# Convolution-offset sampling, attention and expert layer on one core: a one-sided row ramp, two alternating PSUM pairs, transposed exponentials, and elementwise work moved between engines

## The chip, the cores and the metric

The kernel runs on one core of one Trainium2 chip. The metric is the device time of one execution in microseconds (us): the median of three runs of the kernel before is 10409.05 us (10402.94 to 10426.91). The engines of the core are named as in the profile: PE is TensorE (PEld its weight loads, which overlap the matmuls), DVE is VectorE, ACT is ScalarE, POOL is GpSimd, and SP issues the DMAs.

## What is computed

The input is 16 images of 64 x 64 pixels with 128 channels. Layer 0 normalises groups of four channels, computes two offsets for every channel and pixel with a 3 x 3 convolution, and reads the normalised image at the shifted place by bilinear interpolation; the result is added to x. Layer 1 is an attention inside each token (eight heads of 16 numbers, a 16 x 16 score matrix for each head) and a layer of 64 experts, each of which takes its eight best tokens of the image.

```python
coords = off + grid                       # per channel and pixel: row c0, column c1
c0, c1 = clip(coords[0], 0, 63), clip(coords[1], 0, 63)
mapped = bilinear(group_norm(x), c0, c1)  # four neighbours, weights from the fractions
x = x + mapped
q, k, v = heads(layer_norm(x) @ w_qkv + b_qkv)
attn = softmax((q * scale)[..., :, None] * k[..., None, :], axis=-1)
x = x + einsum('bhlij,bhlj->bhli', attn, v) @ w_proj + b_proj
x = x + experts(layer_norm(x))            # top 8 tokens of each of 64 experts
```

## The kernel before

`image` (line 1034) emits the work of one image: image 0 by itself, images 1 to 14 as a hardware loop (line 1070), and image 15 by itself; `finish` then runs the experts. Each image has 256 steps (`SLOTS`), that is 128 pairs of steps. All work of an image is first recorded as a list of operations, each with a slot (its due step), and `order` (line 237) then plays the engines through with estimated costs (`weight`, line 194) and fixes the order of each engine's queue. The order in a queue is thus set when the program is built; on the chip an instruction only waits for its operands. The cost rule knows that a DVE operation with two SBUF operands, or an SBUF-to-SBUF scalar or copy operation, can't run beside POOL (`shared`, line 224).

Sampling (`sample`, line 685), for each pair `p`: four DMAs bring the column coordinates into `chat` (`load_cols`); two bf16 matmuls write row arguments into `rps` (`spread_rows`); two ACT passes turn them into row weights `rhat`, a Relu of the argument and then a Relu of 1 minus it (`ramp_rows`; every eighth pair takes one DVE instruction instead); ACT makes the column weights in place (`ramp_cols`); 64 small matmuls multiply the rows held in `xr` with `rhat` into `yps` (`mains`); DVE multiplies `yps` with `chat` into `prod` (`product`); and each second pair, eight matmuls add up `prod` in `acc` (`sums`). `rps` and `yps` are one pair of PSUM banks each; `acc`, `bank`, `bank2` and `cbank` are the other four banks. `chat` has four buffers, `rhat` three, `prod` three.

`prep` (line 505) makes the next image ready while the present one is sampled: statistics, `normalize` into `pad` (DVE), differences along the columns into `big` (`along`, two DVE instructions), and differences down the rows into the staging buffers `xl` (`down`, eight DVE instructions), from which DMAs write `xn_d` in HBM. `load_rows` (line 601) brings `xn_d` back into `xr` with 32 DMAs for an image. They can be issued once all of `xn_d` is written and the sampling has done with `xr`.

`tokens` (line 795) runs the attention for 512 tokens at a time, eight times an image. For each of four token groups: `qkv_mm` and `qkv_add`; `ends` finds the largest and the smallest key of a head (DVE); `scores` multiplies both with q (POOL, into `top` and `den`); a DVE maximum of the two is the largest score (line 904). Then, in two halves: `score` (two POOL instructions), `expo` (ACT exponential in place and DVE sum), `weigh` (POOL multiplies with v into the one buffer `ev`, DVE sums). `proj` multiplies with `w_proj`; POOL has added `b_proj` to the residual before (line 897). `layer_norm` (line 768) scales with four DVE instructions into `xln` where it feeds the experts.

Of the kernel before, what the change touches and what calls it, by code (L numbers as in the profile page):

```python
# [9 lines left out]
F32 = mybir.dt.float32  # L10
# [9 lines left out]
P = 128  # L20
# [12 lines left out]
REACH = 10.0  # L33
ROW0 = (0, 12, 20, 32)
# [3 lines left out]
NCHAT, NRHAT, NPROD = 4, 3, 3  # L38
# [102 lines left out]
class Work:  # L141
# [52 lines left out]
    def weight(self, op):  # L194
        total, cells, shape = 0, {}, None
        for fn, outs, ins in op.operands():
# [14 lines left out]
            elif op.lane == "gpsimd":  # L211
                total += 1000 if n <= NA else 150 + (6 if fn == "tensor_scalar" else 1.8) * n
# [89 lines left out]
class Images:  # L302
# [8 lines left out]
    def __init__(self, ctx, tc, x, conv_w, conv_b, w_qkv, b_qkv, w_proj, b_proj, gate_w, gate_b,  # L311
# [14 lines left out]
        self.rps = ps.tile([P, 2, 512], F32, name="rps")  # L326
        self.yp = ps.tile([P, 2, CHW], F32, name="yps")
        self.ys = [self.yp[:, 0, :], self.yp[:, 1, :]]
# [49 lines left out]
        self.one = keep([P, 1], "one")  # L378
        nc.vector.memset(self.one, 1.0)
# [16 lines left out]

        id16 = keep([16, 16], "id16", BF16)
# [8 lines left out]
        srow = keep([1, 2, WIN], "srow")  # L406
        nc.vector.tensor_scalar(srow[:, 0], self.iot[0:1, :WIN], -1.0, None, ALU.mult)
        nc.vector.tensor_scalar(srow[:, 1], self.iot[0:1, :WIN], 1.0, None, ALU.add)
        line = self.big.bitcast(BF16)[0:1, 6144:].rearrange("p (r t c) -> p r t c", r=2, t=8)
        self.sel = [keep([P, 8, P], f"sel{o}", BF16) for o in range(2)]  # L410
        for o in range(2):
            sel = self.sel[o].rearrange("p t (a h i) -> p t a h i", a=2, h=2)
            for a in range(2):
                for h in range(2):
                    nc.vector.tensor_scalar(
                        sel[:, :, a, h], bcast(pat[:, 16 * a + h : 16 * (a + 1) : 2], 2, WIN),
                        (1.0, -1.0)[o], None, ALU.mult)
            nc.vector.tensor_copy(
                line[:, 0].rearrange("p t (q i) -> p (t q) i", i=WIN),
                bcast(srow[:, o], 1, 32))  # L420
            nc.vector.memset(line[:, 1], (-1.0, 1.0)[o])
# [67 lines left out]
        self.rstd = [keep([P, NA], f"rstd{i}") for i in range(2)]  # L489
        self.qkv = keep([P, NA, 3, C], "qkv")  # L490
# [5 lines left out]
        self.ev = keep([P, 4, HD, HD], "ev")  # L496
# [8 lines left out]
    def prep(self, b, turns, slot, norm_slot):  # L505
# [41 lines left out]
        def group5():  # L547
# [3 lines left out]
            nc.gpsimd.tensor_tensor(gmv[:, 3:4], gmv[:, 3:4], self.half[:, 0:1], ALU.pow)  # L551

# [3 lines left out]
        def normalize(t):  # L556
            nc.vector.tensor_scalar(
                self.pad[:, 1 + 8 * t : 9 + 8 * t, 1 : 1 + IMG],
                self.big[:, CHW * t : CHW * (t + 1)].rearrange("p (i j) -> p i j", j=IMG),
                gmv[:, 2:3], gmv[:, 3:4], ALU.subtract, ALU.mult,  # L560
            )
# [6 lines left out]
        def along(s):  # L568
            if s == 0:
                nc.vector.tensor_tensor(  # L570
                    big[:, :, : mid - 1], pin[:, :, : mid - 1], pin[:, :, 1:mid], ALU.subtract)
                nc.scalar.copy(big[:, :, mid - 1 : mid + 1], pin[:, :, mid - 1 : mid + 1])
            else:
                nc.vector.tensor_tensor(
                    big[:, :, mid + 1 :], pin[:, :, mid + 1 :], pin[:, :, mid : IMG - 1],
                    ALU.subtract)

        def down(r):
            st = self.xl[:, r % 2].rearrange("p a c -> p (a c)").rearrange(
                "p (i j) -> p i j", j=IMG)  # L580
# [694 lines left out]
```

## Time and profile before

The profiled execution took 10408.53 us; its span, from the first to the last instruction, is 10406.5 us. The program divides so (times from the start of the span):

| stretch, us | what runs | length, us |
|---|---|---|
| 0 to 82 | constants, preparation of image 0 | 82 |
| 82 to 655 | image 0 | 573 |
| 655 to 9185 | loop over images 1 to 14 | 14 x 609 |
| 9185 to 9790 | image 15 | 605 |
| 9790 to 10406 | `finish` | 616 |

POOL's first instruction of a loop pass starts at 1264.34 us and, twelve passes later, at 8578.33 us, which makes 609.5 us for an image. The groups of instructions in one pass (4914.3 to 5525.0 us) that the change bears on, each with its count, its busy time in that pass and the mean of one:

| engine, tile | count | busy us | mean ns |
|---|---|---|---|
| ACT second pass rhat<-rhat,one | 112 | 128.6 | 1148 |
| ACT first pass rhat<-rps | 112 | 113.5 | 1013 |
| DVE rhat<-rps | 16 | 19.4 | 1216 |
| DVE pad<-big,gmv | 8 | 6.3 | 846 |
| DVE big<-pad | 2 | 4.5 | 2258 |
| DVE xl<-big | 8 | 12.2 | 1672 for seven, 615 for the last |
| POOL ev<-sc,qkv | 64 | 151.5 | 2367 |
| POOL sc<-sc,top | 64 | 125.8 | 1965 |
| POOL t<-t,bproj | 8 | 11.2 | 1394 |
| PE bank<-wproj,tr | 64 | 10.2 | 307 |

In the profile all of an image's instructions carry line 188, where the recorded operations are emitted; they are told apart by their tiles. `out<-in` names the tile written and those read.

### The profile page before, as it was taken

To read this page: it belongs to the slowest core of one execution; us is meant where nothing else is said; L and a number is where in the kernel's file an instruction comes from. 1 tells how busy PE (TensorE), PEld (TensorE's weight loads), DVE (VectorE), ACT (ScalarE), POOL (GpSimd) and SP (SyncE) were. 2 spreads that over 40 slices of the span, in tenths; PEclk is the share of its full clock that TensorE was granted. 3 is DMA by queue.
4 is the path that set the end of the run, shared out by engine and by line. 5 is a ranking of instruction groups with operands and counts; after the bars stand their busy time and mean duration, and the time that the engine had idled before them with its cause. 6 is when DMAs were issued, how large, how long until landed. Compare 5 with 4: busy or idle time off the path is not lost. (4 is left out here: it accounts for less than half of the span.)

```text
span 10406.5 us, 367626 instructions
## 1 busy us (share of the span) xinstructions
PE 8673.1 (83%) x156228; PEld 4367.3 (42%) x156228; DVE 8475.8 (81%) x11691; ACT 7657.4 (74%) x8034; POOL 7911.5 (76%) x5666
## 2 busy tenths in 40 slices
PE   7978788797878889788888978788897878888567
PEld 3434344343434434343443434344343434434247
DVE  5988889888888988888898888889888888988712
ACT  5878788787878878787887878788787878878500
POOL 3978788787878878787887878788787878878700
PEclk9999899998989999999999999999998999999755
DMA  6565555555555555555555555555555555555277
GB/s 160 160 166 157 159 159 158 160 161 163 158 158 159 153 161 159 163 160 160 158 154 161 159 162 161 158 152 156 164 160 159 162 158 154 157 163 157 79 213 247
DMA packets 1325857, 1672.20 MB, mean 161 GB/s; under 512 B 441632, under 2 KB 658464, under 8 KB 1322080
## 3 DMA queue, kind: packets, MB, share of 16 engines
q1 hardware_dynamic: 1303904, 1613.24, 54.4%
q10 hardware_dynamic: 20224, 34.61, 0.9%
q8 instruction: 1244, 20.38, 0.9%
q14 instruction: 485, 3.97, 0.1%
HBM read 1378.16 MB, written 268.96 MB: 158 GB/s over the span
## 5 line engine op out<-in xcount | busy, mean ns | idle before, releaser
L188 DVE SCALAR_TENSOR_TENSOR prod<-chat,yps 128x1024 f32<-128x1024 f32 x2048 | 2470.7, 1206 | 552.7 <-PE yps L188 254.6
L188 PE MATMUL yps<-rhat,xr 32*32 32x176 f32 (+1 forms) x131072 | 2621.3, 282 | 347.7 <-DVE prod L188 324.8
L188 POOL TENSOR_TENSOR ev<-sc,qkv 128x1024 f32<-128x1024 f32 x1024 | 2429.5, 2373 | 546.3 <-ACT sc L188 484.2
L188 PEld LDWEIGHTS yps<-rhat,xr 32*32 32x32 f32 x131072 | 1860.2, 106 | 1692.0 <-DVE prod L188 926.2
L188 PE MATMUL cbank<-pad,wconv 128*128 128x512 f32 x4608 | 2433.2, 626 | 39.1 <-DVE far L188 15.4
L188 ACT ACTIVATE rhat<-rps 128x1024 f32<-128x1024 f32 x1792 | 1815.9, 1013 | 633.1 <-PE rps L188 526.8
L188 POOL TENSOR_TENSOR sc<-sc,top 128x1024 f32<-128x1024 f32 x1024 | 2010.4, 1963 | 231.6 <-DVE top L188 203.2
L188 ACT ACTIVATE rhat<-rhat,one 128x1024 f32<-128x1024 f32 x1792 | 2057.6, 1148 | 47.1
L188 POOL TENSOR_TENSOR sc<-qkv 128x1024 f32<-128x1024 f32 x1024 | 1987.9, 1942 | 68.9 <-DVE qkv L188 67.6
L188 PE MATMUL rps<-parts,sel 128*128 128x512 bf16 x4096 | 1251.0, 387 | 723.9 <-ACT rhat L188 414.1
L188 DVE TENSOR_REDUCE den<-sc 128x64 f32<-128x1024 f32 x1024 | 1239.8, 1211 | 326.2 <-ACT sc L188 323.0
L188 DVE TENSOR_REDUCE att<-ev 128x64 f32<-128x1024 f32 x1024 | 1233.3, 1204 | 314.1 <-PEq L1070 265.8
L188 ACT ACTIVATE sc<-sc 128x1024 f32<-128x1024 f32 x1024 | 1071.7, 1047 | 497.9 <-PEq L1070 315.1
L188 ACT ACTIVATE chat<-chat,cbi,csc 128x1024 f32<-128x1024 f32 x1024 | 1255.6, 1232 | 125.8 <-DMA chat<-cc_d 108.8
L188 ACT ACTIVATE chat<-chat,cbi 128x1024 f32<-128x1024 f32 x1024 | 1161.4, 1139 | 183.8 <-DMA chat<-cc_d 162.5
L188 PE MATMUL acc<-prod,red 128*32 128x512 f32 x8192 | 1155.4, 629 | 8.5 <-DVE prod L188 8.5
L188 PEld LDWEIGHTS cbank<-pad,wconv 128*128 128x128 f32 x4608 | 828.4, 193 | 692.6 <-issue 468.1
L188 PEld LDWEIGHTS <-sel 128*128 128x128 bf16 x4096 | 334.3, 98 | 1819.4 <-issue 1564.2
L188 POOL TENSOR_TENSOR top<-qkv,kmm 128x128 f32<-128x128 f32 x512 | 226.2, 442 | 692.0 <-POOLq L1070 359.1
L188 DVE TENSOR_SCALAR xln<-t,mv,rstd 128x128 f32<-128x128 f32 x512 | 530.0, 1094 | 41.8 <-POOL rstd L188 41.8
L188 PE MATMUL bank<-wqkv,tr 128*128 128x384 f32 x1024 | 487.3, 561 | 30.8 <-ACT tr L188 18.1
L188 DVE RECIPROCAL den<-den 128x128 f32<-128x128 f32 x512 | 480.0, 937 | 4.5
(143 smaller groups left out, 8134.9 us busy)
## 6 DMA issues: line engine op xcount, KB each, us to landing
chat<-cc_d SPq DMA_DIRECT2D x8192, 128.0 KB
xr<-xn_d SPq DMA_DIRECT2D x512, 128.0 KB
xn_d<-xl SPq DMA_DIRECT2D x192, 256.0 KB
pc_d<-pc SPq DMA_DIRECT2D x128, 384.0 KB
parts<-pc_d SPq DMA_DIRECT2D x768, 64.0 KB
xl<-in_x_dram SPq DMA_DIRECT2D x128, 256.0 KB
xres<-in_x_dram SPq DMA_DIRECT2D x256, 128.0 KB
cc_d<-cd SPq DMA_DIRECT2D x128, 256.0 KB
```

The lines of the kernel that those rows point to most:

```text
L188: getattr(engine, fn)(*args, **kwargs)
```

## The change

1. Rows: before, a row's weight is 1 minus the distance to it, cut to between 0 and 1, by way of a ramp that is cut at both ends, and `xn_d` holds first differences down the rows. After, a row window of 32 is described from its middle (`MID` = 16): one row is held whole, the two first differences beside it, and for the rest second differences, each difference with a ramp that is cut at zero alone. `ramp_rows` is one ACT Relu for every pair; `by_vector` is never true.
2. Banks: `rps` and `yps` become two pairs of PSUM banks, taken in turn by the pairs; a pair's row arguments and, after them, its products are written to the same banks. `rhat` has two buffers.
3. Preparation: `normalize` goes from DVE to ACT, `along` from DVE to POOL, and `down` is replaced by `first` (eight POOL instructions, in place) and `second` (eight POOL instructions into the staging buffers), with `middle` and `sides` for the rows at the middle. Two small POOL instructions are added for the mean times the scale.
4. Layer norm: `scale` goes from DVE to ACT, with two small POOL instructions added.
5. Attention: the smallest key is subtracted from the keys (`shift`, POOL), so that the largest score is the Relu of q times the largest shifted key (`tops`, POOL, then ACT). `expo` writes its result transposed, so that `ev` is laid out by key and then by query; `weigh` works in place on it, and the two DVE sums read it with a step of 16 numbers. `ev` has two buffers.
6. `b_proj` is added by four matmuls in `proj`, and the POOL addition is dropped.

The general path for far offsets (`general`, line 1078) keeps the old differences with `dense`; it isn't taken with these inputs.

```diff
+MID = 16
...
-NCHAT, NRHAT, NPROD = 4, 3, 3
+NCHAT, NRHAT, NPROD = 4, 2, 3
...
-                total += 1000 if n <= NA else 150 + (6 if fn == "tensor_scalar" else 1.8) * n
+                total += 1000 if n <= NA else 150 + (6 if fn == "tensor_scalar" else 1.75) * n
...
-        self.rps = ps.tile([P, 2, 512], F32, name="rps")
-        self.yp = ps.tile([P, 2, CHW], F32, name="yps")
-        self.ys = [self.yp[:, 0, :], self.yp[:, 1, :]]
+        self.yps = [ps.tile([P, 2, CHW], F32, name=f"yps{i}") for i in range(2)]
...
+        srow = self.big[0:1, 2304:2432].rearrange("p (o i) -> p o i", o=4)
+        nc.vector.memset(srow[:, 0, :1], 0.0)
+        nc.vector.memset(srow[:, 0, 1 : MID + 1], -1.0)
+        nc.vector.memset(srow[:, 0, MID + 1 :], 1.0)
+        nc.vector.memset(srow[:, 1], 1.0)
+        nc.vector.tensor_scalar(srow[:, 3], self.iot[0:1, :WIN], -1.0, None, ALU.mult)
+        nc.vector.memset(srow[:, 2, :1], 1.0)
+        nc.vector.tensor_copy(srow[:, 2, 1 : MID + 1], self.iot[0:1, 1 : MID + 1])
+        nc.vector.tensor_scalar(srow[:, 2, MID + 1 :], srow[:, 3, MID + 1 :], 1.0, None, ALU.add)
...
-                    nc.vector.tensor_scalar(
+                    nc.vector.tensor_tensor(
                         sel[:, :, a, h], bcast(pat[:, 16 * a + h : 16 * (a + 1) : 2], 2, WIN),
-                        (1.0, -1.0)[o], None, ALU.mult)
...
+                        bcast(fac[:, o], 1, 8), ALU.mult)
...
+        self.nmr = keep([P, NA], "nmr")
...
-        self.ev = keep([P, 4, HD, HD], "ev")
+        self.ev = [keep([P, 4, HD, HD], f"ev{i}") for i in range(2)]
...
             nc.gpsimd.tensor_tensor(gmv[:, 3:4], gmv[:, 3:4], self.half[:, 0:1], ALU.pow)
+            nc.gpsimd.tensor_scalar(gmv[:, 2:3], gmv[:, 2:3], -1.0, None, ALU.mult)
+            nc.gpsimd.tensor_tensor(gmv[:, 2:3], gmv[:, 2:3], gmv[:, 3:4], ALU.mult)
         for i, fn in enumerate((group1, group2, group3, group4, group5)):
             plan.add(slot + i + 0.5 * (i % 2), fn)
         def normalize(t):
-            nc.vector.tensor_scalar(
+            nc.scalar.activation(
                 self.pad[:, 1 + 8 * t : 9 + 8 * t, 1 : 1 + IMG],
                 self.big[:, CHW * t : CHW * (t + 1)].rearrange("p (i j) -> p i j", j=IMG),
-                gmv[:, 2:3], gmv[:, 3:4], ALU.subtract, ALU.mult,
-            )
+                AF.Identity, bias=gmv[:, 2:3], scale=gmv[:, 3:4])
...
             if s == 0:
-                nc.vector.tensor_tensor(
+                nc.gpsimd.tensor_tensor(
                     big[:, :, : mid - 1], pin[:, :, : mid - 1], pin[:, :, 1:mid], ALU.subtract)
                 nc.scalar.copy(big[:, :, mid - 1 : mid + 1], pin[:, :, mid - 1 : mid + 1])
             else:
-                nc.vector.tensor_tensor(
+                nc.gpsimd.tensor_tensor(
                     big[:, :, mid + 1 :], pin[:, :, mid + 1 :], pin[:, :, mid : IMG - 1],
                     ALU.subtract)
+        def stage(r):
+            return self.xl[:, r % 2].rearrange("p a c -> p (a c)").rearrange(
+                "p (i j) -> p i j", j=IMG)
         def down(r):
-            st = self.xl[:, r % 2].rearrange("p a c -> p (a c)").rearrange(
...
+            st, lo, hi = stage(r), 8 * r, 8 * (r + 1)
             last = hi == IMG
             nc.vector.tensor_tensor(
                 st[:, : 8 - last], big[:, lo : hi - last], big[:, lo + 1 : hi + 1 - last],
@@ -591,9 +611,45 @@
                 if lo <= w + WIN - 1 < hi:
                     nc.sync.dma_start(self.xn_d[:, WIN - 1, n], big[:, w + WIN - 1])
+        def middle():
+            for n, w in enumerate(ROW0):
+                nc.sync.dma_start(self.xn_d[:, 0, n], big[:, w + MID])
+        def first(r):
+            lo, hi = 8 * r, min(8 * (r + 1), IMG - 1)
+            nc.gpsimd.tensor_tensor(
+                big[:, lo:hi], big[:, lo:hi], big[:, lo + 1 : hi + 1], ALU.subtract)
+        def sides():
+            st = stage(0)
+            for n, w in enumerate(ROW0):
+                nc.sync.dma_start(self.xn_d[:, MID, n], big[:, w + MID - 1])
+                nc.scalar.mul(st[:, n], big[:, w + MID], -1.0)
+            nc.sync.dma_start(self.xn_d[:, MID + 1], st[:, :4])
+        def second(r):
+            st, lo, hi = stage(r + 1), max(8 * r, 1), min(8 * (r + 1), IMG - 1)
+            nc.gpsimd.tensor_tensor(
+                st[:, : hi - lo], big[:, lo - 1 : hi - 1], big[:, lo:hi], ALU.subtract)
+            for n, w in enumerate(ROW0):
+                for i0, i1, at in ((w + 1, w + MID, w), (w + MID + 1, w + WIN - 1, w - 1)):
+                    i0, i1 = max(lo, i0), min(hi, i1)
+                    if i0 < i1:
+                        nc.sync.dma_start(
+                            self.xn_d[:, i0 - at : i1 - at, n], st[:, i0 - lo : i1 - lo])
         for t in range(NCH):
             plan.add(norm_slot + t // 2, lambda t=t: normalize(t))
-            plan.add(norm_slot + 6 + 2 * t, lambda t=t: down(t))
+            if dense:
+                plan.add(norm_slot + 6 + 2 * t, lambda t=t: down(t))
+            else:
+                plan.add(norm_slot + 6 + t // 2, lambda t=t: first(t))
+                plan.add(norm_slot + 10 + 1.5 * t, lambda t=t: second(t))
+        if not dense:
+            plan.add(norm_slot + 5.5, middle)
+            plan.add(norm_slot + 9.5, sides)
         for s in range(2):
             plan.add(norm_slot + 4 + s, lambda s=s: along(s))
         return plan
@@ -681,10 +737,9 @@
...
         def by_vector(p):
-            return p % 8 == 3
+            return False
...
                 nc.tensor.matmul(
-                    self.rps[:, e, :], self.sel[by_vector(p)][:, t, :],
+                    self.yps[p % 2][:, e, :], self.sel[0][:, t, :],
                     self.parts[k % 2][:, m, :], start=True, stop=True)
...
         def ramp_rows(p):
             r = rhat[p % NRHAT]
             if by_vector(p):
-                nc.vector.tensor_scalar(r, self.rps, 0.0, 1.0, ALU.max, ALU.min)
+                nc.vector.tensor_scalar(r, self.yps[p % 2], 0.0, None, ALU.max)
             else:
-                nc.scalar.activation(r, self.rps, AF.Relu)
-                nc.scalar.activation(r, r, AF.Relu, bias=self.one, scale=-1.0)
+                nc.scalar.activation(r, self.yps[p % 2], AF.Relu)
...
                         nc.tensor.matmul(
-                            ys[e][v : v + 32, lo:hi],
+                            self.yps[p % 2][v : v + 32, e, lo:hi],
                             xr[t][g : g + 32, m, n, window(k) : window(k) + WIN],
                             rhat[p % NRHAT][g : g + 32, e, lo:hi], start=True, stop=True)
...
-                prod[p % NPROD], chat[p % NCHAT], 1.0, self.yp, ALU.min, ALU.mult)
+                prod[p % NPROD], chat[p % NCHAT], 1.0, self.yps[p % 2], ALU.min, ALU.mult)
...
+            if dst is not None:
+                nc.gpsimd.tensor_scalar(self.nmr, mv[:, :, 0], -1.0, None, ALU.mult)
+                nc.gpsimd.tensor_tensor(self.nmr, self.nmr, rstd, ALU.mult)
         def scale(a):
-            nc.vector.tensor_scalar(
-                dst[:, a, :], src[:, a, :], mv[:, a, 0:1], rstd[:, a : a + 1],
-                ALU.subtract, ALU.mult,
-            )
+            nc.scalar.activation(
+                dst[:, a, :], src[:, a, :], AF.Identity, bias=self.nmr[:, a : a + 1],
+                scale=rstd[:, a : a + 1])
...
-        def ends(a):
-            for i in range(2):
-                nc.vector.tensor_reduce(
-                    tile_of(self.kmm[:, i, :], a), heads(1, a), AX.X, ALU.min if i else ALU.max)
-        def scores(a):
-            for i, ap in enumerate((top, den)):
-                nc.gpsimd.tensor_tensor(
-                    tile_of(ap, a), heads(0, a), bcast(tile_of(self.kmm[:, i, :], a), 2, HD),
-                    ALU.mult)
+        def end(a, i):
+            nc.vector.tensor_reduce(
+                tile_of(self.kmm[:, i, :], a), heads(1, a), AX.X, ALU.max if i else ALU.min)
+        def shift(a):
+            nc.gpsimd.tensor_tensor(
+                heads(1, a), heads(1, a), bcast(tile_of(self.kmm[:, 0, :], a), 2, HD),
+                ALU.subtract)
+        def tops(a):
+            nc.gpsimd.tensor_tensor(
+                tile_of(top, a), heads(0, a), bcast(tile_of(self.kmm[:, 1, :], a), 2, HD),
+                ALU.mult)
...
+            return self.sc[i % 2], self.ev[i % 2], [heads(s, a)[:, hs] for s in range(3)], [
...
+        def by_query(ap):
+            return ap.rearrange("p h j i -> p h i j")
...
         def expo(i):
-            sc, _, (_, ds, _) = group(i)
-            nc.scalar.activation(sc, sc, AF.Exp)
+            sc, ev, _, (_, ds, _) = group(i)
+            nc.scalar.activation(by_query(ev), sc, AF.Exp)
             plan.slot += 1
-            nc.vector.tensor_reduce(ds, sc, AX.X, ALU.add)
+            nc.vector.tensor_reduce(ds, by_query(ev), AX.X, ALU.add)
         def weigh(i):
-            sc, (_, _, vs), (_, _, at) = group(i)
-            nc.gpsimd.tensor_tensor(self.ev, sc, bcast(vs, 2, HD), ALU.mult)
+            _, ev, (_, _, vs), (_, _, at) = group(i)
+            nc.gpsimd.tensor_tensor(ev, ev, bcast(vs, 3, HD), ALU.mult)
             plan.slot += 2
-            nc.vector.tensor_reduce(at, self.ev, AX.X, ALU.add)
+            nc.vector.tensor_reduce(at, by_query(ev), AX.X, ALU.add)
...
-        add(14, lambda: nc.gpsimd.tensor_tensor(t1, t1, bcast(self.bproj, 1, NA), ALU.add))
...
-            add(at + 9, lambda: ends(a))
-            add(at + 10, lambda: scores(a))
-            add(at + 11, lambda: nc.vector.tensor_tensor(
-                tile_of(top, a), tile_of(top, a), tile_of(den, a), ALU.max))
+            add(at + 9, lambda: end(a, 0))
+            add(at + 9.5, lambda: shift(a))
+            add(at + 10, lambda: end(a, 1))
+            add(at + 10.5, lambda: tops(a))
+            add(at + 11, lambda: nc.scalar.activation(tile_of(top, a), tile_of(top, a), AF.Relu))
...
-                nc.tensor.matmul(self.bank[:, P * a : P * (a + 1)], attT[:, a, :], self.wproj,
-                                 start=True, stop=True)
+                ps = self.bank[:, P * a : P * (a + 1)]
+                nc.tensor.matmul(ps, self.ident, self.bproj, start=True, stop=False)
+                nc.tensor.matmul(ps, attT[:, a, :], self.wproj, start=False, stop=True)
```

## The prediction

> **What bounds the kernel now.** The loop comes first: 14 passes and the images before and after them fill 9,700 of the 10,406 us, and `finish` isn't touched. The first view is the busy time of each engine in one pass, between two restarts of POOL's queue (length, then busy us and count of each engine, granted clock, DMA share, GB/s).
>
> ```profile
> core 0: us, PE busy (x) PEld busy (x) DVE busy (x) ACT busy (x) POOL busy (x), PEclk, DMA share, GB/s
> 4914.30:5525.00 610.70, 520.00 (x9652) 253.99 (x9652) 524.02 (x716) 477.69 (x501) 494.39 (x353) 0.93 0.56 159
> ```
>
> No engine is full: DVE 86%, PE 85%, POOL 81%, ACT 78%. Four engines of nearly one load, each with a fixed order, hold each other up. So I read next whom PE, then POOL, waits for in this pass (total us, times, longest).
>
> ```profile
> PE rps L188 <- ACT rhat L188: 26.6, 34, 3.1
> PE rps L188 <- PEq L1070: 19.3, 1, 19.3
> PE yps L188 <- DVE prod L188: 19.0, 29, 2.5
> PE bank L188 <- DVE xln L188: 12.8, 12, 1.7
> PE bank L188 <- ACT tr L188: 6.2, 8, 2.2
> ```
>
> ```profile
> POOL ev L188 <- ACT sc L188: 29.7, 17, 3.9
> POOL top L188 <- POOLq L1070: 28.2, 1, 28.2
> POOL top L188 <- DVE kmm L188: 20.6, 6, 5.4
> POOL sc L188 <- DVE top L188: 13.3, 23, 1.9
> ```
>
> PE idles 90.7 us: 19.3 at the loop's end, 71.4 inside. Of the 71.4, 58.4 are three waits that the change touches: row arguments for ACT, products for DVE, transposes for the layer norm. The order of time at the loop's end explains the 19.3 (start, length, what):
>
> ```profile
> 5499.85 0.56 SPq L188 DMA_DIRECT2D xn_d<-big  x1
> ...
> 5502.62 17.17 SPq L188 DMA_DIRECT2D xr<-xn_d  x32
> ...
> 5505.28 1.05 PE L188 MATMUL acc<-prod,red 128*32 128x512 f32 x4 [0.47 <-DVE prod L188]
> ...
> 5525.32 1.01 PE L188 MATMUL rps<-parts,sel 128*128 128x512 bf16 x2 [18.99 <-PEq L1070]
> ```
>
> The last rows of the next image leave for `xn_d` only as the pass ends, so all 32 loads of `xr` are issued behind the last product. `down` is due at slots 215 to 229 of 256 and comes late; its DVE instructions, as others with two SBUF operands, are long where POOL is busy (mean ns behind the bar):
>
> ```profile
> L188 DVE TENSOR_SCALAR xln<-t,mv,rstd 128x128 f32<-128x128 f32 x32 | 34.3, 1130 | 3.1 <-POOL rstd L188 3.1
> L188 DVE TENSOR_TENSOR top<-top,den 128x128 f32<-128x128 f32 x32 | 21.0, 655 | 0.0
> L188 DVE TENSOR_TENSOR xl<-big 128x512 f32<-128x512 f32 x7 | 11.6, 1672 | 0.0
> L188 POOL TENSOR_TENSOR cd<-cd,pc 128x512 f32<-128x512 f32 x8 | 9.7, 1207 | 4.5 <-ACT pc L188 4.5
> ```
>
> The third takes 686 ns in the first 90 us of the span, with POOL idle, and the shortest of the first 332.
>
> **The change, part by part, for one pass.**
>
> DVE loses 16 row ramps (19.4), the layer norm's scaling (34.3), the maximum (21.0), `normalize` (6.3), `along` (4.5) and `down` (12.2): 524.0 − 97.7 = 426.3 us.
>
> ACT loses 112 second passes (128.6) and takes 16 first ones (16 × 1.013 = 16.2). For the rest I use its rows: an exponential of 1024 elements takes 1047 ns, a cast of 512 608, hence 0.857 ns an element; a scale read from memory adds 93 (`chat` with `csc` 1232, without 1139). `normalize`: 8 × (608 + 93) = 5.6. Scaling 128 elements: 1047 − 896 × 0.857 = 279, and 186 for two such operands: 32 × 0.465 = 14.9. The Relu on `top`: 32 × 0.279 = 8.9. `sides`: 0.9. Sum 477.7 − 128.6 + 46.5 = 395.6 us.
>
> POOL: `weigh` loses its second full operand and becomes like sc<-sc,top, whose second operand is one number repeated over the inner axis: 64 × (1965 − 2367) = −25.7; the bias addition goes, −11.2. `along` comes: 2 × 1984 × 2.31 (ev<-sc,qkv, also two full operands) = 9.2; `first` and `second`: 16 × 1.207 = 19.3. The small ones: 8 × (0.23 + 0.4), bounded by 0.23 and 1.04 for the second (the two rstd rows), with 1.1 for the image's mean: 6.1. `shift` and `tops` replace two multiplications of their size: 0. Sum 494.4 − 2.3 = 492.1 us.
>
> PE: four more matmuls in `proj`, as many as now cost 10.2: 530.2 us. SP: `xn_d` is written by 29 DMAs where 22 did it, 7 × about 0.5 us of issue; SP waits for products already, so I take nothing, and 3.5 us with that cover gone. `first` overwrites rows that `middle`'s DMAs still read; behind it in POOL's queue stand the scores of the attention. `down` today waits up to 3.8 us for such a DMA (first 90 us), so up to four such waits cost 0 to 15 us of POOL's slack; 0 taken, since the queue's order reckons with 5 us for a DMA (line 291).
>
> Three costs have no row. (a) The transposed exponential and the two sums step 64 bytes through `ev`. From below: 0, as the copy wconv<-big reads every second word at 1348 ns for 1152 elements, 1.17 ns each, and the sum den<-sc, read contiguously, takes 1.18. From above: PE's transposes load weights from every fourth word of `tr` in 209 ns where contiguous ones take 140; these 69 ns over 128 columns, 0.54 an element, would add 0.55 us to each of 128 sums (DVE 497) and 64 exponentials (ACT 431). I take 0: DVE's own row is nearest. (b) Waits inside the pass: nothing of the three may stay (13.0 left of 71.4) or all (71.4). Row arguments no longer wait for ACT but for the product two pairs back, and `mains` for one ACT pass where two ran; queued behind a held `spread_rows` on PE are convolution and token matmuls. With DVE and ACT at some 70% I take 25 of the 58.4, so 38 in all. (c) The loop's end: POOL's `second` needn't wait for a gap in POOL. If `xn_d` is whole when the last 32 steps begin, only the last loads, 8 of 32 (17.17 × 8/32 = 4.3), and the 5.2 us from SP's last issue to the restart remain, some 9.5; I take 12, between 6 and 21.
>
> *Against the change* speaks the Trainium skill, page "Vector Engine (DVE) Microarchitecture Reference", section "5.2 Measured stream behaviour on trn2": a port keeps its full rate only for runs of two adjacent words, and single words hopping cost 1.7 to 2.5 ns a column in two-source programs. By that an estimate of a sum is 1.9 to 2.7 us, DVE goes to 510 to 610 us, and the pass at the upper end gets longer than it is. The wconv row, single words 8 bytes apart at full rate, doesn't bear the rule out; no row steps 64 bytes.
>
> **Sum.** Inside a pass: waits −33.4, PE +10.2, net −23.2, for 16 images −371. Loop's end: −7.3 at 15 changes of image, −110. Before image 0 nothing hides the preparation: normalising +2, `along` +5, `first` +10, partly under DMAs: +15 (0 to 25). 10,408.5 − 466 = 9,942; the median stands 0.5 above the profiled run: 9,943. With (b) at 26 to 50 and (c) at 8 to 19, the forecast's own range is 9,680 to 10,250.
>
> **The rivals.**
>
> *POOL sets the end.* It keeps 492 us, and its chain grows: smallest key, `shift`, largest key, `tops`, Relu, score, where two DVE and two POOL instructions ran back to back. If its 88.1 us of inner waits stay, a pass takes 492.1 + 88.1 + 20.9 = 601.1: −154 + 15, thus 10,270. Against: 29.7 and 13.3 of the waits are for ACT and DVE, which lose load, and `ev` has two buffers.
>
> *More than forecast.* PE's waits shrink to 20, the end to 8, and the slow matmuls that follow a wait (9 of 128 groups of products at 1.87 us, the rest at 1.23) go, −10: 548 a pass, about 9,425. For: 25 us stretches with PE busy 24.7 exist. Against: `bank` and `cbank` stay single.
>
> *Strided sums, slower.* Place: the 128 sums over `ev`. At double time each adds 1.18 us: DVE 577; at the share DVE reaches today between the ends (524.0 of 591.4, 0.886) this makes 651, with 12 for the end 663, +52 a pass: 11,260. It decides from DVE's 524 on, 0.76 us more a sum. Against: row (a).
>
> *The alternation gives nothing.* One bank pair now passes through arguments 0.6, Relu 1.0, `mains` 1.23 and product 1.2, 4.0 us, and four hand-offs, for two pairs of steps. Today a pair takes 591/128 = 4.62 us; with 1.3 us lost at each hand-off, the length of one foreign instruction, the ring alone gives 9.2 us for two pairs, and the time stays near 10,400.
>
> **How the numbers follow.** Forecast 0.56, POOL 0.16, more 0.10, strided 0.11, alternation 0.07 (of which 0.04 within 0.2%, 0.02 slower, 0.01 faster; 0.2%, 21 us, is about what a measurement can tell). Faster 0.83, within 0.04, slower 0.13. The range 9,520 to 10,330 holds the forecast and the POOL case and leaves out the strided case and half of the largest gain.
>
> **What would show it.** DVE near 426 us a pass, ACT 396, POOL 492, PE 530; second passes gone; ev<-ev at 1.94 to 1.97 us, the sums still at 1.21 and the exponential at 1.05; no wait of row arguments for `rhat`, a small one for `prod`; most `xr` loads issued before the last product, restart gap under 15 us. I am wrong if the sums take over 1.9 us, if POOL's waits for `kmm` and `top` grow by what PE's shrink, or if the 32 loads still stand in one block at the end.

## The result, and the profile after

The change makes the kernel slower: 10,688.1 us (median of 4 runs, 10,681.33 to 10,691.87) against 10,405.99 us for the kernel before in the same session. The ratio is 1.027 (1.0249 to 1.029). The forecast was 9,943 us, on the other side. The profiled execution took 10,681.33 us, its span 10,679.5 us; six passes of the loop take 3,753.7 us, so one takes 625.6 us where 609.5 were needed.

One pass, between two restarts of POOL's queue, in the same view as before (length, then busy us and count of each engine, granted clock, DMA share, GB/s):

```profile
core 0: us, PE busy (x) PEld busy (x) DVE busy (x) ACT busy (x) POOL busy (x), PEclk, DMA share, GB/s
4443.90:5068.80 624.90, 516.33 (x9716) 255.61 (x9716) 523.36 (x618) 450.88 (x481) 486.00 (x381) 0.95 0.58 155
```

DVE has 98 instructions less than before (618 for 716) and the same work, 523.4 us for 524.0. ACT has lost 27 us of the 82 that it was to lose. POOL is near its forecast (486 for 492), and PE lies below its own (516 for 530). So the prices of DVE's and ACT's remaining instructions went up. Their rows in this pass show which (count, then busy us and mean ns, then idle time of the engine ahead of them and what ended it):

```profile
L189 ACT ACTIVATE ev<-sc 128x1024 f32<-128x1024 f32 x64 | 126.2, 1973 | 51.5 <-PEq L1136 31.9 <-POOL sc L189 18.2 <-DVE att L189 1.0
L189 POOL TENSOR_TENSOR ev<-ev,qkv 128x1024 f32<-128x1024 f32 x64 | 125.2, 1956 | 49.0 <-DVE den L189 48.0 <-DVE ntop L189 0.6
L189 DVE TENSOR_REDUCE den<-ev 128x64 f32<-128x1024 f32 x64 | 121.9, 1904 | 25.4 <-ACT ev L189 25.3
L189 DVE TENSOR_REDUCE att<-ev 128x64 f32<-128x1024 f32 x64 | 121.8, 1903 | 40.2 <-PEq L1136 31.9 <-POOL ev L189 8.2
```

Each sum takes 1.90 us where it took 1.204 and 1.211: 128 × 0.69 = 89 us, about all that DVE was relieved of. Each exponential takes 1.97 us where it took 1.047: 64 × 0.93 = 59 us. These are the instructions that step 64 bytes through `ev`. POOL's product with v, which does not step, came out as forecast (1.96 us).

What PE waits for in this pass, and then POOL (total us, times, longest):

```profile
PE yps L189 <- PEq L1136: 32.9, 1, 32.9
PE yps L189 <- DVE prod L189: 32.4, 38, 3.8
PE yps L189 <- ACT rhat L189: 20.0, 34, 1.7
PE bank L189 <- ACT xln L189: 5.5, 3, 5.0
```

```profile
POOL ev L189 <- DVE den L189: 48.0, 30, 3.9
POOL sc L189 <- POOLq L1136: 25.5, 1, 25.5
POOL top L189 <- DVE kmm L189: 23.8, 20, 4.8
```

PE idles 32.9 us at the loop's end (19.3 before) and 624.9 − 516.3 − 32.9 = 75.7 us inside the pass (71.4 before). Its wait for ACT and for the layer norm fell; that for DVE's products rose from 19.0 to 32.4. The two waits have also changed places, as the rows of the two kinds of matmul show: before, the row arguments waited for ACT and `mains` for DVE; now the row arguments wait until DVE's product has read the shared banks, and `mains` wait for ACT's row weights.

```profile
L189 PE MATMUL yps<-parts,sel 128*128 128x512 bf16 x256 | 78.3, 388 | 66.2 <-PEq L1136 32.9 <-DVE prod L189 32.4 <-DMA parts<-pc_d 0.6
L189 PE MATMUL yps<-rhat,xr 32*32 32x176 f32 x4096 | 144.0, 316 | 20.2 <-ACT rhat L189 20.0
```

POOL now stands 48.0 us for DVE's first sum: the weighing of a half works in place, so it can start only behind the sum that reads the same buffer. Before, it wrote to another buffer and had no such wait. Both waits, PE's for the products and POOL's for the sum, lead to DVE. The order of time at the end of the pass, of SP, PE and POOL (start, length, what, idle time ahead of it):

```profile
5030.83 12.85 SPq L189 DMA_DIRECT2D xn_d<-xl  x10
5046.33 16.82 SPq L189 DMA_DIRECT2D xr<-xn_d  x32
...
5023.27 1.05 PE L189 MATMUL acc<-prod,red 128*32 128x512 f32 x4 [3.01 <-DVE prod L189]
5069.15 1.01 PE L189 MATMUL yps<-parts,sel 128*128 128x512 bf16 x2 [33.22 <-PEq L1136]
...
5040.71 2.35 POOL L189 TENSOR_TENSOR xl<-big 128x512 f32<-128x512 f32 x2
5068.84 1.93 POOL L189 TENSOR_TENSOR sc<-qkv 128x1024 f32<-128x1024 f32 x1 [25.79 <-POOLq L1136]
```

The last products are summed at 5024. POOL works on until 5043; its last two instructions are two of `second`. Only then do the last rows leave for `xn_d`, and the 32 loads of `xr` still stand in one block, from 5046 to 5063, 5.7 us ahead of the restart at 5068.84.

### The profile page after: what moved, and what is told of

Read it like the earlier page. It is cut to its first block, busy times and chain, and to the rows that moved or that the text cites. A ratio compares the mean times of both kernels' runs of the same rounds, so it can differ in the third digit from the quotient of the medians.

```text
span 10679.5 us, 369502 instructions
## 1 busy us (share of the span) xinstructions
PE 8668.1 (81%) x157254; PEld 4396.1 (41%) x157254; DVE 8516.8 (80%) x10130; ACT 7232.2 (68%) x7714; POOL 7777.9 (73%) x6114
## 5 line engine op out<-in xcount | busy, mean ns | idle before, releaser
L189 PE MATMUL yps<-rhat,xr 32*32 32x176 f32 (+1 forms) x131072 | 2535.7, 276 | 322.9 <-ACT rhat L189 306.9
L189 ACT ACTIVATE rhat<-yps 128x1024 f32<-128x1024 f32 x2048 | 2090.4, 1024 | 1016.1 <-PE yps L189 965.1
L189 POOL TENSOR_TENSOR ev<-ev,qkv 128x1024 f32<-128x1024 f32 x1024 | 1995.4, 1949 | 807.0 <-DVE den L189 775.7
L189 PE MATMUL cbank<-pad,wconv 128*128 128x512 f32 x4608 | 2480.7, 636 | 114.2 <-DVE far L189 88.4
L189 ACT ACTIVATE ev<-sc 128x1024 f32<-128x1024 f32 x1024 | 2020.3, 1973 | 782.4 <-PEq L1136 417.8
L189 DVE TENSOR_REDUCE att<-ev 128x64 f32<-128x1024 f32 x1024 | 1950.2, 1905 | 590.0 <-PEq L1136 416.9
L189 DVE TENSOR_REDUCE den<-ev 128x64 f32<-128x1024 f32 x1024 | 1951.8, 1906 | 426.0 <-ACT ev L189 423.0
L189 PE MATMUL yps<-parts,sel 128*128 128x512 bf16 x4096 | 1259.4, 390 | 1047.2 <-DVE prod L189 549.7
L189 DVE SCALAR_TENSOR_TENSOR qkv<-bank,rstd,bqkv 128x384 f32<-128x384 f32 x512 | 311.7, 609 | 235.6 <-PE bank L189 235.6
L189 PEld LDWEIGHTS acc<-prod,red 128*32 128x32 f32 x8192 | 165.2, 109 | 551.6 <-issue 480.6
```

What stands on the lines that cost most here:

```text
L189: getattr(engine, fn)(*args, **kwargs)
```

## The experiments

Each time is a median (four runs, one for the probe) beside the kernel before on the same chip, whose medians were 10,410 to 10,415 us. An edit is against the changed kernel unless it says otherwise.

**1. `ev` by query again.** Only the layout of `ev` goes back; two buffers, the work in place and everything else stay.

```diff
-            nc.scalar.activation(by_query(ev), sc, AF.Exp)
+            nc.scalar.activation(ev, sc, AF.Exp)
...
-            nc.vector.tensor_reduce(ds, by_query(ev), AX.X, ALU.add)
+            nc.vector.tensor_reduce(ds, ev, AX.X, ALU.add)
...
-            nc.gpsimd.tensor_tensor(ev, ev, bcast(vs, 3, HD), ALU.mult)
+            nc.gpsimd.tensor_tensor(ev, ev, bcast(vs, 2, HD), ALU.mult)
...
-            nc.vector.tensor_reduce(at, by_query(ev), AX.X, ALU.add)
+            nc.vector.tensor_reduce(at, ev, AX.X, ALU.add)
```

> The exponentials are written contiguously, by query and then by key; weigh multiplies with v as before the change; nothing else differs from the changed kernel. Stride theory (the 64-byte steps of the exponential and of the two sums fill DVE and ACT up again and hold the pass): sums back at 1.21 us, exponential at 1.05, weigh at 2.37; DVE some 435 us a pass, ACT 392, POOL 512; the time falls below the kernel before, 10,050 to 10,300. End theory (the pass is held by the late rows of the next image, 33 us of bubble at the loop's end): the engines get as much emptier, but the bubble grows by part of what the sampling gains, and the time stays between 10,400 and 10,650. Ring theory (the shared banks hold the pass): 10,550 or more, with the waits of the row arguments for the product still above 30 us a pass.

Measured: 10,071.28 us, ratio 0.9678 (0.9662 to 0.9694). This is the fastest kernel here, ahead of both. One pass, its rows and PE's waits:

```profile
4764.60:5352.50 587.90, 498.48 (x9614) 254.47 (x9716) 442.68 (x619) 400.95 (x482) 511.31 (x382) 0.95 0.63 165
```

```profile
L189 POOL TENSOR_TENSOR ev<-ev,qkv 128x1024 f32<-128x1024 f32 x64 | 152.3, 2379 | 15.5 <-DVE den L189 14.2 <-DVE ntop L189 0.8
L189 DVE TENSOR_REDUCE den<-ev 128x64 f32<-128x1024 f32 x64 | 77.4, 1209 | 11.0 <-ACT ev L189 10.8
L189 ACT ACTIVATE ev<-sc 128x1024 f32<-128x1024 f32 x65 | 68.4, 1052 | 85.7 <-PEq L1136 64.2 <-POOL sc L189 21.2
```

```profile
PE yps L189 <- PEq L1136: 32.8, 1, 32.8
PE yps L189 <- ACT rhat L189: 17.0, 33, 1.7
PE yps L189 <- DVE prod L189: 15.7, 17, 2.8
```

The queues of DVE, ACT, POOL and SP hold the same instructions in the same order as in the changed kernel, since the planner's costs don't know the steps; so the difference of 617 us is the price of the layout and nothing else. It is the price of the steps less POOL's gain: by query, the weighing costs POOL 27 us more a pass (2.38 for 1.96 us). PE's wait for DVE's products halves, POOL's for the sum falls from 48.0 to 14.2 us. The loop's end stays at 32.8 us. (PE has 9,614 matmul records here where it has 9,716 weight loads: 102 matmuls of row arguments are missing from the trace, so its busy time is too low.)

**2. Only the sums step.** The scores are made by key in the first place, so the exponential is contiguous and only the two sums step 64 bytes.

```diff
-            nc.gpsimd.tensor_tensor(sc, bcast(qs, 3, HD), bcast(ks, 2, HD), ALU.mult)
-            nc.gpsimd.tensor_tensor(sc, sc, bcast(ts, 3, HD), ALU.subtract)
+            nc.gpsimd.tensor_tensor(sc, bcast(qs, 2, HD), bcast(ks, 3, HD), ALU.mult)
+            nc.gpsimd.tensor_tensor(sc, sc, bcast(ts, 2, HD), ALU.subtract)
...
-            nc.scalar.activation(by_query(ev), sc, AF.Exp)
+            nc.scalar.activation(ev, sc, AF.Exp)
```

> The scores themselves are computed by key and then by query, so that the exponential reads and writes contiguously and only the two sums step by 64 bytes; one of POOL's score instructions then has two full operands (2.37 us where it took 1.96). Stride theory with DVE as the holder: exponential 1.05 us, sums still 1.90, DVE still 523 us a pass, the time stays within 60 us of the changed kernel's 10,688. With ACT's long exponential as the holder: the time falls by more than half of what the contiguous layout gains. End and ring theories: within 60 us of 10,688.

Measured: 10,538.55 us, ratio 1.0128 (1.0111 to 1.0145). Two rows of its pass:

```profile
L189 POOL TENSOR_TENSOR sc<-sc,top 128x1024 f32<-128x1024 f32 x64 | 152.9, 2390 | 2.0 <-ACT top L189 0.9
L189 DVE TENSOR_REDUCE den<-ev 128x64 f32<-128x1024 f32 x64 | 121.8, 1903 | 9.2 <-ACT ev L189 9.2
```

POOL's load is that of the first experiment (512.8 for 511.3 us), as the slower price moved from the weighing to the subtraction; the exponential is at 1.053 us in both. So the two sums alone cost 10,538.6 − 10,071.3 = 467 us. The stepped exponential makes up the other 150, with a POOL that has 27 us less to do a pass; its price with POOL's load held was not measured. None of the expectations was met: the time left the 60 us around 10,688, but fell by less than half of 617.

**3. The step by itself.** Ahead of everything else DVE, ACT and POOL run, three times each, a sum, an exponential that writes with steps, one that reads with steps, and a product, all of 1024 elements, at steps of 1, 2, 4, 8, 16 and 64 words. This is extra work, and the kernel's whole time is not read.

```diff
+        for w in (1, 2, 4, 8, 16, 64):
+            def hop(ap):
+                return ap.rearrange("p (h j i) -> p h i j", j=16, i=w)
...
+                nc.vector.tensor_reduce(sums(probe[:, 4000:4064]), hop(probe[:, :1024]), AX.X, ALU.add)
...
+                nc.scalar.activation(hop(probe[:, 2048:3072]), flat(probe[:, 1024:2048]), AF.Exp)
...
+                nc.gpsimd.tensor_tensor(flat(probe[:, 2048:3072]), hop(probe[:, 1024:2048]), hop(probe[:, 1024:2048]), ALU.mult)
```

> The changed kernel with a few extra instructions on scratch data ahead of everything: a DVE sum of 1024 elements, an ACT exponential that writes, one that reads, and a POOL product that reads with steps of 1, 2, 4, 8, 16 and 64 words. Stride theory: the DVE sum takes 1.2 us at one word and at two words, and 1.9 at 16; the exponential 1.05 at one word and 1.97 when it writes at 16 words; at which step it sets in is open. If instead contention with other engines made them long in the pass, they take 1.2 and 1.05 us here at every step.

The order of time: one DVE sum each at 1, 2, 4 and 16 words (L357), then three ACT exponentials together at the same steps (L359, the writes):

```profile
5.18 1.22 DVE L357 TENSOR_REDUCE big<-big 128x64 f32<-128x1024 f32 x1
...
9.29 1.21 DVE L357 TENSOR_REDUCE big<-big 128x64 f32<-128x1024 f32 x1
...
13.13 1.96 DVE L357 TENSOR_REDUCE big<-big 128x64 f32<-128x1024 f32 x1
...
28.01 1.74 DVE L357 TENSOR_REDUCE big<-big 128x64 f32<-128x1024 f32 x1
```

```profile
5.18 3.23 ACT L359 ACTIVATE big<-big 128x1024 f32<-128x1024 f32 x3 [3.14 <-DVE big L345]
17.63 3.44 ACT L359 ACTIVATE big<-big 128x1024 f32<-128x1024 f32 x3 [5.95 <-POOL big L363]
30.61 6.20 ACT L359 ACTIVATE big<-big 128x1024 f32<-128x1024 f32 x3 [6.01 <-POOL big L363]
...
68.50 5.82 ACT L359 ACTIVATE big<-big 128x1024 f32<-128x1024 f32 x3 [6.38 <-POOL big L363]
```

A step of 2 words is free for DVE and costs ACT 7%. From 4 words on both are slow: DVE 1.74 to 2.01 us, ACT 1.94 to 2.07, reads with steps as slow as writes. So for DVE and ACT, reading and writing SBUF, the cost comes with the step, with its edge between 8 and 16 bytes, and not from two engines meeting at one buffer. POOL's three products together take 5.83 us at 1 word and at most 6.59, at 4 words, so POOL is nearly indifferent:

```profile
11.76 5.83 POOL L363 TENSOR_TENSOR big<-big 128x1024 f32<-128x1024 f32 x3 [9.15 <-DVE big L357]
...
43.13 6.59 POOL L363 TENSOR_TENSOR big<-big 128x1024 f32<-128x1024 f32 x3 [12.56 <-ACT big L361]
```

**4. POOL's weighing with its operands exchanged**, in the kernel of experiment 1 (`bcast(vs, 2, HD), ev` for `ev, bcast(vs, 2, HD)`), to see what makes 2.38 us.

> e1_ev_by_query with the two operands of weigh exchanged (v first, the exponentials second), the same product. If the order of the operands decides between POOL's 2.37 and 1.95 us, POOL falls from 511 to some 485 us a pass; then, if POOL's share of the pass holds the end (it works on for some 25 us after the last products in e1), the time falls to 9,750 to 9,950, and if it doesn't, to no less than 10,000. If the order is indifferent, weigh stays at 2.37 and the time within 30 us of 10,071.

Measured: 10,085.09 us, ratio 0.9686 (0.967 to 0.9702); the weighing takes 2.369 us. The order of the operands doesn't matter. Experiment 2's subtraction takes 2.39 us where a full operand meets a row of 16 different numbers repeated, and 1.93 to 1.96 where it meets one number repeated over the inner axis; in the probe a full operand with itself takes 1.94 us and more. But the repeated row by itself isn't slow: the product of q and k has such a row beside a repeated number and takes 1.94 us, here in the kernel of experiment 1. What makes the 2.38 us stays open.

```profile
L189 POOL TENSOR_TENSOR sc<-qkv 128x1024 f32<-128x1024 f32 x65 | 125.7, 1935 | 54.0 <-POOLq L1136 51.6 <-ACT ev L189 0.5
```

**5. Is it the loop's end?** The preparation's late part is placed 60 slots earlier in the planner's order, first with all its engines and SP's DMAs, then with POOL's instructions alone, then POOL's alone in the kernel of experiment 1.

```diff
-                i = min(when, key=lambda i: (when[i] + 150 * ops[i].slot, i))
+                i = min(when, key=lambda i: (when[i] + 150 * (ops[i].slot - ops[i].early), i))
```

> The differences and copies of the next image (normalize to second, with their DMAs) are given a priority 60 slots ahead of their due time when the queues are ordered; the instructions are those of the changed kernel. End theory: the rows of the next image are in HBM before the last product, the loads of xr no longer stand in one block at the end, PE's wait at the loop's end falls from 33 to under 15 us and the time to 10,350 to 10,480. Stride theory: the wait at the end falls too, but the waits inside the pass grow by most of it, 10,580 or more.

Measured: 11,268.91 us, ratio 1.0826 (1.0808 to 1.0845). SP's queue and PE's waits:

```profile
5215.33 80.19 SPq L192 DMA_DIRECT2D xn_d<-xl  x21
```

```profile
PE yps L192 <- DVE prod L192: 95.5, 43, 60.7
PE yps L192 <- PEq L1140: 3.7, 1, 3.7
```

The end is gone (3.7 us for 32.9): the rows were whole in time, and `xr` was loaded in eight groups of four. But SP's queue is in order, the 21 row DMAs stood in it for 80 us waiting for POOL's rows, the loads of `chat` stood behind them, and PE waited for DVE's products for 60.7 us at a stretch. The time lies in the range of the stride theory, but the stall in SP's queue is in neither theory.

> As e3_prep_early, but only POOL's instructions of the preparation get the earlier priority (60 slots); SP's DMAs keep their due time, so that no column load is queued behind a row that isn't ready. Strided steps stay. End theory: PE's wait at the loop's end falls from 33 us to under 15, and the time to 10,350 to 10,480. Stride theory: DVE (523 us a pass) and the order behind it take back most of it, 10,560 or more.

Measured: 10,900.51 us, ratio 1.0464 (1.0447 to 1.0482). PE's end wait is 22.6 us, ten less, and the pass 643.4 us, 18 more.

> e1_ev_by_query and e5_pool_early together. If the steps and the end are two costs that add, the end's bubble goes from 33 to under 15 us a pass and the time from 10,071 to 9,750 to 9,870. If POOL (511 us of 588) is by now what holds the pass, pulling its rows forward only moves the scores of the attention back: 10,000 or more.

Measured: 10,304.17 us, ratio 0.9888 (0.9871 to 0.9904), 233 us slower than experiment 1; the end takes 23.0 us. Only some of the rows are made early. POOL has two staging buffers for them and waits 10.3 us for the DMAs that empty them; from 4847 to 4859 us those DMAs stand in SP's queue behind a store of token results, and the last of `second` comes at 4872 us, 5 us before POOL's end. POOL's token work fills the time between: POOL is busy 19.9 of the 20 us from 4840 while PE falls to 6.3.

**6. `second` back on DVE**, in the kernel of experiment 1 (`nc.vector` for `nc.gpsimd`).

> e1_ev_by_query with the second differences on DVE, where down was before the change. If the late rows come from POOL's load at the end of the pass (it is busy 27 to 29 of each 30 us there in e1), the bubble shrinks and the time falls to 9,850 to 9,990. If they come from the chain itself (staging buffers, DMAs, due slots), or if DVE's wait for POOL makes them as late as down was, the time stays within 60 us of 10,071.

Measured: 10,082.57 us, ratio 0.9681 (0.9665 to 0.9697). POOL has 6.7 us less to do, DVE 7.5 more, the end takes 30.3 us, and the time is 11 us (0.1%) above that of experiment 1.

**7. The alternation of banks.** A pair keeps one pair of banks for arguments and one for products (`self.yps[0]` and `self.yps[1]` for `self.yps[p % 2]`), in the changed kernel, then in that of experiment 1; last, the kernel before gets the alternation alone.

> Row arguments and products have a bank pair each, as before the change, instead of taking turns; the rest is the changed kernel. Ring theory: the row arguments no longer wait for the product, and the time falls by 200 us or more. Stride and end theories: the time stays within 80 us of 10,688 or rises, since the products of two pairs can no longer overlap.

> e1_ev_by_query with a bank pair for arguments and one for products, as in e4_own_banks. With the strided steps, own banks cost 170 us. If the alternation is worth that for itself, 10,180 to 10,320; if it only helps where DVE is full, under 10,130.

> The kernel before with the two pairs of PSUM banks taken in turn by the pairs of steps, and nothing else: two ACT passes a pair, three row buffers. If the alternation is good by itself, the row arguments no longer wait for ACT (26.6 us a pass) nor the products for DVE (19.0): 10,150 to 10,330. If the ring of four hand-offs costs what the alternation saves while ACT and DVE are full: 10,380 or more.

Measured: 10,858.44 us, ratio 1.0432 (1.0414 to 1.0449); 10,220.99 us, ratio 0.9813 (0.9796 to 0.9829); and 10,632.66 us, ratio 1.0212 (1.0195 to 1.0229). So the alternation is worth 170 us in the changed kernel and 150 in that of experiment 1, where PE's waits for ACT's row weights and DVE's products are together 32.7 us with it and 43.4 without. Alone it makes the kernel before 2.1% slower: the two waits grow from 45.6 to 57.3 us, of which `mains` wait 37.5 for the row weights. There two ACT passes still lie between a pair's arguments and the products that need its banks; that this is the reason is argued, not shown. All three have queues of another order than their base, which is part of these numbers.

**8. The moves of SBUF work off DVE.** In the kernel of experiment 1, `normalize` and the layer norm's scaling go back to DVE, and the four small POOL instructions that served them go.

```diff
-            nc.scalar.activation(
-                dst[:, a, :], src[:, a, :], AF.Identity, bias=self.nmr[:, a : a + 1],
-                scale=rstd[:, a : a + 1])
+            nc.vector.tensor_scalar(
+                dst[:, a, :], src[:, a, :], mv[:, a, 0:1], rstd[:, a : a + 1],
+                ALU.subtract, ALU.mult,
+            )
```

> e1_ev_by_query with normalize and the layer norm's scaling on DVE again, as before the change, and without the four small POOL instructions for them. If these moves are worth what the forecast took (room on DVE, no waiting for POOL), xln is near 1.1 us again, PE's waits for it return to some 13 us a pass, and the time rises by 100 to 250 us. If they were worth little once DVE has room, it stays within 60 us of 10,071.

Measured: 10,517.49 us, ratio 1.0106 (1.0089 to 1.0122), 446 us slower than experiment 1. Two of PE's waits in its pass:

```profile
PE yps L189 <- PEq L1133: 30.3, 1, 30.3
PE bank L189 <- DVE xln L189: 28.1, 14, 10.4
```

The wait for the layer norm, 4.7 us with ACT, is 28.1 with DVE, up to 10.4 at a time, and the scaling takes 1.26 us a piece where ACT takes 0.48. DVE's load rises by 42 us, and the pass by 28.7 (616.6 for 587.9). The 446 us are more than either theory gave. The queues' order changed too, so they are these moves and what the planner makes of them.

## Why the prediction was wrong

**The step that failed is (a), the strided steps, taken at 0.** The prediction had two rows. One was DVE's own, a copy that reads every second word at full rate; the other was PE's, weight loads from every fourth word, slower by 0.54 ns an element. I chose by engine, and the step mattered more: the probe shows that 2 words are free for DVE and 4 are not, so the DVE row said nothing of 16. Even the upper end was too low: 0.55 us for a sum that takes 0.69 more, and for an exponential that takes 0.93 more. That no row stepped as far was not so either. One in three of ACT's copies from `bank` to `tr`, the one ahead of the experts, reads PSUM with a step of 128 words, and all of these copies take about the same (ns, least, median, most):

```profile
L188 ACT COPY tr<-bank x384: 561/578/596, 171.4 to 9849.3; 128x512 f32<-128x512 f32 x192
```

That row would have said 0 for ACT, but it is a read of PSUM, and the exponential's step lies in SBUF. So the rows of before said 0, 0.54 ns and 0, and no safe upper end could be worked out from them. DVE came out at 523 us for 426, ACT at 451 for 396, and the kernel lost 617 us by it, more than the whole forecast gain of 466.

**The rival "strided sums, slower" had the mechanism and the place**; only its price was too high. It doubled the sum (1.18 us more, 11,260), measured are 0.69. Its rule held well: DVE reaches 523.4 / (624.9 − 32.9) = 0.884 of the time between the ends, where the rival took 0.886 from the trace of before. Its point of decision, DVE's 524, is where DVE ended; that the pass got 16 us longer there, and not 0, lies mostly in the loop's end, 13.6 us longer, which the rival had put 7.3 us shorter. The exponential, to which it gave no price, holds DVE's share down: without its step, in experiment 2, DVE reaches 527.3 / (614.4 − 33.3) = 0.907.

The rule of the Trainium skill ("Vector Engine (DVE) Microarchitecture Reference", section "5.2 Measured stream behaviour on trn2") gave an estimate of 1.9 to 2.7 us for a sum; the sums took 1.90. For single words 8 bytes apart, where it would have the slow rate too, the probe's 1.21 us agrees with the wconv row and not with it.

**(c), the loop's end, failed too**, by 21 us a pass: 32.9 us where 12 were taken, above the upper bound of 21. That POOL's `second` needn't wait for a gap was right, but it has no priority in POOL's queue either: its last two instructions are POOL's last of the pass, 19 us behind the last products, and the 32 loads stand in one block behind them. This term costs 21 × 15 = 315 us of the forecast, if an end can be had at 12. Experiments 5 and 6 don't get it: with everything pulled forward the end falls to 3.7 us, but a longer stall inside takes its place; with POOL's rows alone pulled forward it falls to 23, and the rest of the pass grows by more; with `second` on DVE it stays at 30. My reading, argued and not shown, is that POOL has a fixed load for a pass and SP's order decides the rest. Which order of SP and POOL would shorten the end without a stall inside was not found, and stays open.

**(b), the waits inside, was too low by 9 us a pass.** Taken were 38 us of 71.4; in the changed kernel they are 75.7. What they are without the steps can be read in experiment 4, which differs from experiment 1 by the order of two operands alone and has all matmuls on record:

```profile
4188.00:4773.10 585.10, 505.09 (x9716) 252.37 (x9716) 441.89 (x618) 400.17 (x482) 510.98 (x382) 0.96 0.63 166
PE yps L189 <- PEq L1136: 33.0, 1, 33.0
```

That leaves 585.1 − 505.1 − 33.0 = 47.0 us. "No wait of row arguments for `rhat`" came true: the 20.0 and 17.0 us for `rhat` are waits of `mains`. The row arguments' wait for `prod`, forecast as small, is 32.4 us in the changed kernel and 15.7 in experiment 1.

**The other terms.** With (a) taken out, the forecast misses by 128 us (10,071 for 9,943), 1.3%. That it is so little is luck. Worked out were 530.2 + 38 + 12 = 580.2 us a pass; experiment 4 has 505.1 + 47.0 + 33.0 = 585.1. Waits and end were taken 30 us too short and PE's busy time 25 us too long, at a granted clock of 0.96 for 0.93. The forecast left PE's matmuls at their price of before; the rival "more than forecast" had put their shortening, at 10 us. It had also put the waits at 20 us and the end at 8, and neither came. ACT's casts and scalings were priced well: 450.9 less the exponentials' 59 is 392, forecast 396. DVE is at 442.7 in experiment 1, forecast 426.3. Of these 16.4 us, 6.5 are two instructions left on DVE with SBUF operands that take longer (the scaling of `cd` 1.26 us for 0.92, the expert's `big<-big,logits` 1.15 for 0.67). That a busier POOL holds them up is not shown: in the changed kernel POOL is busy 486 of 625 us where it was 494 of 611, and `big<-big,logits` still takes 0.93. POOL's total came out 6 us lower, with `along` at 3.58 us for 4.6. The weighing lost 0.41 us as forecast, but not for the reason given: v was never a full operand but a row of 16 numbers repeated, and two full operands are no slower than its new form (1.94 us in the probe, where both are the same one). The same misreading had priced `along`.

**The remaining rivals.** POOL does not hold the pass in the changed kernel: its 48.0 us wait for DVE's sum speaks for DVE. In experiment 1 it comes near: 511 of the 555 us between the ends, with a wait for DVE of 14 us. That the alternation gives nothing is refuted for the changed kernel and for experiment 1, where it gives 1.5%; by itself, on the kernel before, it takes 2.1%. Not tested by themselves are the two buffers of `rhat` where there were three, the weighing in place, and the one-sided ramp.

## What to carry to other kernels

Price a changed access pattern by a row of the same engine, in the same memory and with the same step. If there is none, rows of another engine or a smaller step are no price: here they said 0 and 0.54 ns an element, and DVE paid 0.67, ACT 0.90 and POOL nothing. Give such a step a wide range and a test of its own ahead of the forecast. A layout that suits one engine is paid for by every other engine that reads or writes it: here POOL gained 27 us a pass and DVE and ACT paid 148. And parts of one change are worth what the other parts make of them: the bank alternation costs 2.1% alone and gives 1.5% in the kernel of experiment 1, so measure them one by one on top of the rest.

## What was not expected of the hardware

- In SBUF the edge lies between 8 and 16 bytes: DVE's sum of 1024 elements takes 1.21 us at 4 and 8 bytes, 1.96 at 16, 2.00 at 32, and then a little less, 1.74 to 1.89 at 64 bytes and 1.79 to 1.80 at 256. ACT's exponential does the same, 1.08, 1.15, 2.07, 2.05, 1.94 and 1.95 us, whether the step is in what it reads or in what it writes. ACT's copies of 512 elements out of PSUM don't show it: with a step of 512 bytes and without, they take 561 to 596 ns.
- POOL's product is at 1.94 to 2.2 us at every one of these steps, but takes 2.37 to 2.39 us where a full operand meets a row of 16 numbers repeated, on either side. Such a row beside a repeated number takes 1.94.
